# The tail of an AdaLN block: Sinkhorn renewed from exponent bits with its kernels in PSUM, branch output and residual added on GpSimd, ten of sixteen mix steps on TensorE

## The chip, the core and the metric

The kernel runs on one core of one Trainium2 chip. Five engines share the work: TensorE (PE in the profile) multiplies matrices into PSUM, VectorE (DVE), ScalarE (ACT) and GpSimd (POOL) work elementwise, and SyncE (SP) issues most DMA transfers. The metric is the device time of one launch in microseconds (us), the median of several runs. All data is 32-bit float.

## What is computed

The block takes x of 4 batches by 512 tokens by 1024 channels and adds two gated branches to it. The first is a Mamba-like branch (projection, convolution, selective scan, output projection). The second, which the change is about, is this, cut to what matters (C = 256 channels in each of n = 4 streams):

```python
x_norm = x * rsqrt(mean(x * x) + eps)                      # x: the modulated layer norm, "h" below
H_res_logits = (x_norm @ W_res.T).reshape(B, T, 4, 4) + H_res_base
H_res  = sinkhorn_log(H_res_logits)                        # 50 steps, tau = 0.1
H_pre  = softmax(x_norm @ W_pre.T + H_pre_base)
H_post = softmax(x_norm @ W_post.T + H_post_base)
H_res  = (1 - g) * I + g * H_res                           # g = sigmoid(gate)
x_pre  = einsum('btnc,btn->btc', x_streams, H_pre)
y      = x_pre @ W_branch
x_mixed       = einsum('btij,btjc->btic', H_res, x_streams)
y_distributed = einsum('btc,btn->btnc', y, H_post)
out = x + gb * (x_mixed + y_distributed)                   # x: the block's stream after the first branch
```

`sinkhorn_log` alternates u = -logsumexp over columns of Z + v and v = -logsumexp over rows of Z + u, 50 times, for one 4x4 matrix per token.

## The kernel before, in words

The 2048 tokens are 16 tiles of 128 tokens, one token to a partition. Everything up to the first branch's output lies in the first `with` block: eight blocks of 256 tokens, in each a selective scan of 64 steps on VectorE (L963) with TensorE, ScalarE (L933) and GpSimd (L917) feeding it. This part is ordered by hand (`manual_schedule`, L1003). It uses all eight PSUM banks: `ps_ht` 2, `ps_da` 2, `ps_mm` 4 (L104 to L106). `front` (L773) normalizes each tile for the second branch, stores it to DRAM (`h2_dram`) and leaves 24 logits per token in `lgs`: 16 for Sinkhorn, 4 for each softmax. The last two tiles' logits come at the very end of this block (L829).

The second `with` block (L1037) is the tail. Here the framework's scheduler orders the instructions of each engine when the kernel is built; an engine then runs its own list strictly in that order, and waits on semaphores for the others. The parts are:

- Loads (L1067, L1070): `h2` and `x1`, 16 tiles of 512 KB each, on SP's queue, and later a row of gb per batch, broadcast to all partitions (`gb_row`, L1047).
- `softmaxes` (L1074): H_pre and H_post.
- `sinkhorn` (L1088): in two parts, tiles 0 to 13 (part 0, tile names `sk`, `sa`, `sb`) and tiles 14 and 15 (part 1, `skl`). Instead of logarithms it scales: with kk = exp(z) and kt its transpose, each of 50 steps is product, row sum and reciprocal for u (L1131, L1132, L1133) and the same for v (L1135, L1136, L1137), six VectorE instructions. After steps 10, 20, 30 and 40 the scales are folded into z: ScalarE takes logarithms (L1140, L1141), VectorE adds them (L1142, L1143) and ScalarE makes kk and kt anew (L1122, L1123). All four tiles z, kk, kt, w lie in SBUF. Part 1 is begun beside part 0 at its step 16 and carried on between the mixes.
- `branch` (L1162), per tile: ScalarE writes four diagonal matrices from H_pre (L1158), TensorE multiplies with them to form x_pre transposed (L1172), then multiplies by W_branch (L1180); ScalarE copies y out (L1182).
- `mix` (L1185), per tile, needs H_res: output streams 0 and 1 on TensorE, ten matmuls with diagonals that ScalarE writes (L1196, L1197: eight for H_res, two for H_post times y); streams 2 and 3 by eight multiply-adds on VectorE into PSUM (L1204), begun from y times H_post by ScalarE (L1202). Then VectorE multiplies by gb (L1210, L1211), GpSimd adds x1 (L1212), SP stores (L1213).

Of the kernel before, what the change touches and what calls it, by code (L numbers as in the profile page):

```python
# [8 lines left out]

F32 = mybir.dt.float32  # L10
AF = mybir.ActivationFunctionType
# [11 lines left out]
TT = TB // P  # L23
# [13 lines left out]
NS, C = 4, 256  # L37
NL = NS * NS + 2 * NS
BT = T // P
NTT = B * BT  # L40
SINKHORN_ITERS = 50
ABSORB = 10
# [3 lines left out]
EPS_LN = 1e-05  # L46
EPS_FFN = 1.1920929e-07
SA, CA, GA, SB, CB, GB = range(6)


@with_exitstack
def adaln_block(
# [22 lines left out]
    vec, act, pool, pe = nc.vector, nc.scalar, nc.gpsimd, nc.tensor  # L75
# [20 lines left out]

    parts_of = [(0, NTT - TT), (NTT - TT, TT)]
    lgs = [const.tile([P, n, NL], F32, name=f"lg_{i}", tag=f"lg_{i}") for i, n in parts_of]
    sk = const.tile([P, 4, parts_of[0][1], NS, NS], F32, name="sk")

    with ExitStack() as ph:
        p1 = ph.enter_context(tc.tile_pool(name="p1", bufs=1))
        p2 = ph.enter_context(tc.tile_pool(name="p2", bufs=2))
# [899 lines left out]
        with tc.manual_schedule():  # L1003
# [5 lines left out]
            for k in range(NBLK):  # L1009
# [27 lines left out]
    with ExitStack() as ph:  # L1037
        p1 = ph.enter_context(tc.tile_pool(name="f1", bufs=1))
        p2 = ph.enter_context(tc.tile_pool(name="f2", bufs=2))
        ps_oa = ph.enter_context(tc.tile_pool(name="ps_oa", bufs=2, space=PSUM))  # L1040
        ps_ob = ph.enter_context(tc.tile_pool(name="ps_ob", bufs=2, space=PSUM))
        ps_tr = ph.enter_context(tc.tile_pool(name="ps_ft", bufs=2, space=PSUM))
        NM = NS // 2

        gbs = {}

        def gb_row(b):  # L1047

            if b not in gbs:
                gbs[b] = p2.tile([P, H], F32, name=f"row_gb_{b}", tag="row_gb")  # L1050
                load(gbs[b], row_dram[GB][b, :].partition_broadcast(P))
            return gbs[b]

# [34 lines left out]
        def sinkhorn(part, tiles):  # L1088

            n = parts_of[part][1]
            sh = [P, n, NS, NS]
            z, kk, kt, w = (tiles[:, m] for m in range(4))

            def small(name):
                return const.tile([P, n, NS], F32, name=f"{name}_{part}", tag=f"{name}_{part}")
# [10 lines left out]
            mx, sa, sb_ = small("mx"), small("sa"), small("sb")  # L1109
            vec.tensor_scalar(  # L1110
                z, lgs[part][:, :, : NS * NS].rearrange("p t (i j) -> p t i j", j=NS), INV_TAU,
                None, ALU.mult,
            )
            vec.tensor_reduce(mx, z, AX.X, ALU.max)
            vec.tensor_tensor(z, z, over_j(mx), ALU.subtract)
            act.activation(w, z, AF.Exp)
            vec.tensor_reduce(sa, w, AX.X, ALU.add)
            vec.tensor_reduce(mx, by_col(z), AX.X, ALU.max)
            vec.tensor_tensor(z, z, over_i(mx), ALU.subtract)

            def kernel_of():
                act.activation(kk, z, AF.Exp)  # L1122
                act.activation(kt, by_col(z), AF.Exp)  # L1123

            kernel_of()
            fresh = False
            for it in range(SINKHORN_ITERS):
                if fresh:
                    vec.tensor_reduce(sa, kk, AX.X, ALU.add)
                elif it:  # L1130
                    vec.tensor_tensor(w, kk, over_i(sb_), ALU.mult)  # L1131
                    vec.tensor_reduce(sa, w, AX.X, ALU.add)  # L1132
                vec.reciprocal(sa, sa)  # L1133

                vec.tensor_tensor(w, kt, over_i(sa), ALU.mult)  # L1135
                vec.tensor_reduce(sb_, w, AX.X, ALU.add)  # L1136
                vec.reciprocal(sb_, sb_)  # L1137
                fresh = it and it % ABSORB == 0
                if fresh:
# [6 lines left out]
            hr = kk  # L1146
            vec.tensor_tensor(w, w, over_j(sb_), ALU.mult)
            vec.tensor_scalar(hr, by_col(w), gt, None, ALU.mult)
            dg = hr.rearrange("p t i j -> p t (i j)")[:, :, 0 : NS * NS : NS + 1]
            vec.tensor_scalar(dg, dg, gm, None, ALU.add)  # L1150
# [9 lines left out]
        ybs = {}  # L1160

        def branch(i):  # L1162

            hpp = own(hpps, i)
            dg = p1.tile([P, NS, P], F32, name=f"dgx_{i}", tag="dgx", bufs=3)
            xt = ps_tr.tile([P, C // P, P], F32, name=f"pxt_{i}", tag="xt")
# [11 lines left out]
            py = ps_tr.tile([P, C], F32, name=f"pyb_{i}", tag="yb")  # L1178
            for j in range(C // P):
                pe.matmul(py, xs[:, j, :], wbr[:, j, :], start=(j == 0), stop=(j == C // P - 1))  # L1180
            yb = p1.tile([P, C], F32, name=f"yb_{i}", tag="yb", bufs=NTT)
            act.copy(yb, py)  # L1182
            ybs[i] = yb

        def mix(i):  # L1185


            b, r = divmod(i, BT)
            hpp, hres = own(hpps, i), own(hress, i)
            hs = [h2[:, i, n * C : (n + 1) * C] for n in range(NS)]  # L1190
            oa = ps_oa.tile([P, NM, C], F32, name=f"oa_{i}", tag="oa")
            ob = ps_ob.tile([P, NS - NM, C], F32, name=f"ob_{i}", tag="ob")
            dg = p1.tile([P, NM, NS + 1, P], F32, name=f"dg_{i}", tag="dg", bufs=2)
            for n in range(NM):
                for m in range(NS + 1):
                    diagonal(dg[:, n, m, :], hres[:, n, m : m + 1] if m < NS else hpp[:, 1, n : n + 1])  # L1196
                    pe.matmul(  # L1197
                        oa[:, n, :], dg[:, n, m, :], hs[m] if m < NS else ybs[i],
                        start=(m == 0), stop=(m == NS),
                    )  # L1200
            for n in range(NM, NS):
                act.activation(ob[:, n - NM, :], ybs[i], AF.Copy, scale=hpp[:, 1, n : n + 1])  # L1202
                for m in range(NS):
                    vec.scalar_tensor_tensor(  # L1204
                        ob[:, n - NM, :], hs[m], hres[:, n, m : m + 1], ob[:, n - NM, :],
                        ALU.mult, ALU.add,
                    )
            of = p1.tile([P, H], F32, name=f"o_{i}", tag="o", bufs=3)
            gb = gb_row(b)
            vec.tensor_tensor(of[:, : NM * C], oa.rearrange("p n c -> p (n c)"), gb[:, : NM * C], ALU.mult)  # L1210
            vec.tensor_tensor(of[:, NM * C :], ob.rearrange("p n c -> p (n c)"), gb[:, NM * C :], ALU.mult)  # L1211
# [10 lines left out]
        for it in range(SINKHORN_ITERS + 1):  # L1222
            next(early, None)
            if it == APART:
                softmaxes(1)
                for i in last:
                    branch(i)
                small = p1.tile([P, 4, TT, NS, NS], F32, name="skl")
                late = sinkhorn(1, small)
            if late:  # L1230
                next(late, None)
# [56 lines left out]
```

## Time and profile before

| | us |
|---|---|
| median of 3 runs | 2709.85 (2709.05 to 2709.86) |
| the profiled execution's own time | 2702.3 |
| its span, first to last instruction | 2700.5 |
| first Sinkhorn step of part 0 (L1133) | at 2412.6 |
| first diagonal of the tail (L1158) | at 2476.8 |
| first diagonal of the mix | at 2603.8 |
| last addition on GpSimd (L1212) ends | at 2696.8 |

Busy time over the span: PE 2408.1 us (89%), DVE 2361.0 (87%), ACT 1716.9 (64%), POOL 1731.8 (64%). A row of the timeline gives the start in us from the span's start, the time that the merged instructions took, the engine, the source line, the operation with output and inputs, and in brackets how long the engine had been idle before and what ended that. A group gives busy time, mean nanoseconds of one instruction, and idle time with its releasers. A row of the windows table gives busy time and number of instructions per engine in that stretch, the granted TensorE clock (1.00 is full), the DMA share and GB/s.

### The profile page before, as it was taken

How to read it: one execution, taken by the hardware profiler on the slowest of the kernel's cores; microseconds unless marked ns; L12 is line 12 of the kernel's file. 1: busy time of each engine (PE TensorE's matmuls, PEld its weight loads, DVE VectorE, ACT ScalarE, POOL GpSimd, SP SyncE). 2: the span in 40 equal slices, each digit the busy share in tenths (PEclk: the TensorE clock that was granted, in tenths of full speed). 3: DMA queues.
4: the chain of work that ended last, by engine and by line, in shares of the span. 5: the costliest groups of instructions: out<-in, count | busy, mean ns of one | idle time of the engine just before them, and what ended most of it. 6: DMA issues, size and time to landing. Idle time of an engine off the chain costs nothing. (4 is left out here: it accounts for less than half of the span.)

```text
span 2700.5 us, 39703 instructions
## 1 busy us (share of the span) xinstructions
PE 2408.1 (89%) x13392; PEld 2051.6 (76%) x13392; DVE 2361.0 (87%) x4451; ACT 1716.9 (64%) x3755; POOL 1731.8 (64%) x1167
## 2 busy tenths in 40 slices
PE   8999989999999989998999899998999899885446
PEld 8887478888788878887888788887888777675435
DVE  0349898999999999999999999999999899977898
ACT  0356567666776777667776776668666856633445
POOL 0146557777976688768766786779676977931014
PEclk9979989999999999999999999999999899896769
DMA  5432523333433343234333433333333323225302
GB/s 184 152 125 94 204 75 130 113 106 121 154 117 104 116 153 121 106 114 149 125 110 114 156 118 109 118 145 125 121 106 124 130 94 117 83 74 203 153 31 110
DMA packets 74347, 331.06 MB, mean 123 GB/s; under 512 B 8496, under 2 KB 25312, under 8 KB 47456
## 3 DMA queue, kind: packets, MB, share of 16 engines
q1 hardware_dynamic: 62784, 311.56, 32.1%
q10 hardware_dynamic: 11360, 16.96, 1.7%
q8 instruction: 107, 1.75, 0.3%
q14 instruction: 96, 0.79, 0.1%
HBM read 303.14 MB, written 25.35 MB: 122 GB/s over the span
## 5 line engine op out<-in xcount | busy, mean ns | idle before, releaser
L917 POOL TENSOR_TENSOR w<-u,b 128x1024 f32<-128x1024 f32 x512 | 1209.1, 2363 | 558.2 <-PE hq L943 413.5
L933 ACT ACTIVATE da<-dv,aneg 128x256 f32<-128x256 f32 x2048 | 971.5, 477 | 616.5 <-DVE w L963 571.5
L963 DVE TENSOR_TENSOR_SCAN w<-da,w 128x256 f32<-128x256 f32 x2048 | 1263.3, 667 | 69.5 <-ACT da L933 47.6
L952 DVE SCALAR_TENSOR_TENSOR acc<-hq,ss,acc 128x512 f32<-128x512 f32 x1024 | 724.6, 735 | 78.2 <-PE hq L943 73.1
L943 PE MATMUL hq<-ident,w 128*128 128x128 f32 x4096 | 644.1, 282 | 73.1 <-DVE acc L952 53.7
L943 PEld LDWEIGHTS hq<-ident,w 128*128 128x128 f32 x4096 | 511.8, 146 | 220.7 <-issue 57.7
L487 PE MATMUL pz<-w_z,ht 128*128 128x256 f32 x2048 | 517.2, 387 | 0.0
L439 PE MATMUL pp<-ht,w_x 128*128 128x259 f32 x2048 | 511.5, 387 | 0.0
L667 PE MATMUL po<-y,w_out 128*128 128x256 f32 x2048 | 496.2, 381 | 5.4 <-ACT dv L608 5.4
L439 PEld LDWEIGHTS pp<-ht,w_x 128*128 128x128 f32 x2048 | 372.1, 193 | 46.2 <-issue 0.4
L667 PEld LDWEIGHTS po<-y,w_out 128*128 128x128 f32 x2048 | 368.6, 191 | 46.5 <-ACT dv L608 6.9
L487 PEld LDWEIGHTS pz<-w_z,ht 128*128 128x128 f32 x2048 | 369.2, 195 | 36.5 <-issue 0.3
L455 DVE SCALAR_TENSOR_TENSOR xc<-pp,cw,xc 128x256 f32<-128x256 f32 x384 | 178.4, 464 | 31.8 <-ACT xc L448 30.7
L1212 POOL TENSOR_TENSOR o<-o,x 128x1024 f32<-128x1024 f32 x16 | 37.7, 2354 | 189.1 <-ACT dg L1158 142.2
L1197 PE MATMUL oa<-h,dg 128*128 128x256 f32 x256 | 62.8, 389 | 74.9 <-ACT dg L1158 69.5
L1197 PEld LDWEIGHTS oa<-h,dg 128*128 128x128 f32 x256 | 49.3, 195 | 84.1 <-ACT dg L1158 76.5
L467 POOL TENSOR_TENSOR xc<-xc,sx 128x1024 f32<-128x1024 f32 x32 | 75.5, 2358 | 42.8 <-ACT sx L465 42.8
L448 ACT ACTIVATE xc<-pp,cb,cw 128x256 f32<-128x256 f32 x128 | 71.3, 557 | 47.5 <-PE pp L439 47.4
L749 PE MATMUL py<-ident,acc 128*128 128x128 f32 x256 | 48.4, 324 | 54.7 <-ACT dv L608 28.3
L262 PEld LDWEIGHTS pm<-sc,w_mod 128*128 128x128 f32 x384 | 80.9, 323 | 9.0 <-DVE mv_a L358 9.0
L262 PE MATMUL pm<-sc,w_mod 128*128 128x4 f32 x384 | 79.5, 343 | 9.1 <-DMA w_mod<-wmod_dram 9.1
L749 PEld LDWEIGHTS py<-ident,acc 128*128 128x128 f32 x256 | 34.8, 167 | 67.2 <-ACT dv L608 25.2
(172 smaller groups left out, 2303.2 us busy)
## 6 DMA issues: line engine op xcount, KB each, us to landing
w_x<-in_w_dram SPq DMA_DIRECT2D x64, 1024.0 KB, 4.7
w_z<-in_w_dram SPq DMA_DIRECT2D x64, 1024.0 KB, 4.9
w_out<-out_w_dram SPq DMA_DIRECT2D x56, 1024.0 KB, 4.8
w_mod<-wmod_dram SPq DMA_DIRECT2D x24, 1024.0 KB, 4.8
b<-bcd SPq DMA_DIRECT2D x32, 512.0 KB, 3.8
xt<-x_dram SPq DMA_DIRECT2D x16, 512.0 KB, 8.2
xr<-x_dram SPq DMA_DIRECT2D x32, 256.0 KB, 5.1
x<-xr ACTq DMA_DIRECT2D x32, 256.0 KB, 2.5
```

The lines of the kernel that those rows point to most:

```text
L262: pe.matmul(pm[:, 2 * q + j, :], w[:, k, j * P : (j + 1) * P], sc[:, k, :], start=(k == 0), stop=(k == HC - 1),)
L439: pe.matmul(pp, w[:, h, j * P : (j + 1) * P], hts[k][:, h, :], start=(h == 0), stop=(h == HC - 1),)
L455: vec.scalar_tensor_tensor(xc[:, c, :], pp[:, tap : tap + TB], cw[:, i, tap : tap + 1], xc[:, c, :], ALU.mult, ALU.add,)
L487: pe.matmul(pz[:, t, :], hts[k][:, h, PAD + t * P : PAD + (t + 1) * P], w[:, h, :], start=(h == 0), stop=(h == HC - 1),)
L667: pe.matmul(po, w[:, d - lo, :], ys[k, d // QC][:, d % QC, :], start=(d == lo), stop=(d == hi - 1),)
L749: pe.transpose(py[:, j, t * P : (t + 1) * P], acc[:, t, c * P : (c + 1) * P], ident)
L917: pool.tensor_tensor(w, us[k, q], bts[k, n // NG][:, n % NG, :].unsqueeze(1).to_broadcast([P, QC, TB]), ALU.mult,)
L933: act.activation(da[:, j, :], dts[k, q][:, 2 * s + j, :], AF.Exp, scale=aneg[:, i, n : n + 1])
L943: pe.transpose(h[:, c * P : (c + 1) * P], ws[g][:, c, t * P : (t + 1) * P], ident)
L952: vec.scalar_tensor_tensor(acc[:, t, :], hqs.pop((g, t)), cts[k][:, t, n : n + 1], acc[:, t, :], ALU.mult, ALU.add,)
L963: vec.tensor_tensor_scan(w[:, c, :], das[g, c // 2][:, c % 2, :], w[:, c, :], 0.0, ALU.mult, ALU.add)
L1197: pe.matmul(oa[:, n, :], dg[:, n, m, :], hs[m] if m < NS else ybs[i], start=(m == 0), stop=(m == NS),)
```

## The change

Three edits, all in the tail.

**Sinkhorn.** kk and kt move from SBUF to a PSUM tile `kb` from a new pool `ps_kk`; the two scales are halves of one tile `ab`. The renewal takes only the power of two of each scale: VectorE masks the exponent bits (`bits`), turns them into a logarithm by one multiply-add (`low`), adds that to z, and leaves the mantissa of v's scale in place. The step after a renewal is therefore an ordinary one with a product. The result goes to a tile `hr` of its own.

**Branch.** y is no longer kept. ScalarE writes it four times, scaled by H_post, into `yn`; GpSimd multiplies `yn` by gb and adds it to `x1` in place. x_pre and y share one PSUM tile `pb`. The four gb rows have each a buffer of their own.

**Mix.** TensorE does the eight products of streams 0 and 1 and two of stream 2, whose diagonals GpSimd writes; ScalarE does one of stream 3; VectorE does the other five.

```diff
-    sk = const.tile([P, 4, parts_of[0][1], NS, NS], F32, name="sk")
+    sk = const.tile([P, 2, parts_of[0][1], NS, NS], F32, name="sk")
...
+        ps_kk = ph.enter_context(tc.tile_pool(name="ps_kk", bufs=1, space=PSUM))
...
-                gbs[b] = p2.tile([P, H], F32, name=f"row_gb_{b}", tag="row_gb")
+                gbs[b] = p1.tile([P, H], F32, name=f"row_gb_{b}")
...
-            z, kk, kt, w = (tiles[:, m] for m in range(4))
+            z, w = tiles[:, 0], tiles[:, 1]
+            kb = ps_kk.tile([P, 2, n, NS, NS], F32, name=f"kb_{part}", tag=f"kb_{part}")
+            kk, kt = kb[:, 0], kb[:, 1]
...
-                fresh = it and it % ABSORB == 0
-                if fresh:
-                    act.activation(sa, sa, AF.Ln)
-                    act.activation(sb_, sb_, AF.Ln)
-                    vec.tensor_tensor(z, z, over_j(sa), ALU.add)
-                    vec.tensor_tensor(z, z, over_i(sb_), ALU.add)
+                if it and it % ABSORB == 0:
+                    vec.tensor_scalar(bits, ab.bitcast(I32), EXPONENT, None, ALU.bitwise_and)
+                    vec.tensor_scalar(low, bits, LN2 / 2**23, -127 * LN2, ALU.mult, ALU.add)
+                    vec.tensor_tensor(z, z, over_j(low[:, 0]), ALU.add)
+                    vec.tensor_tensor(z, z, over_i(low[:, 1]), ALU.add)
                     kernel_of()
+                    sbi = sb_.bitcast(I32)
+                    vec.tensor_scalar(sbi, sbi, MANTISSA, ONE, ALU.bitwise_and, ALU.bitwise_or)
                 yield
...
-            yb = p1.tile([P, C], F32, name=f"yb_{i}", tag="yb", bufs=NTT)
-            act.copy(yb, py)
-            ybs[i] = yb
+            yn = p1.tile([P, NS, C], F32, name=f"yn_{i}", tag="yn", bufs=3)
+            for n in range(NS):
+                act.activation(yn[:, n, :], py, AF.Copy, scale=hpp[:, 1, n : n + 1])
+            yn = yn.rearrange("p n c -> p (n c)")
+            pool.tensor_tensor(yn, yn, gb_row(i // BT), ALU.mult)
+            pool.tensor_tensor(x1[:, i, :], x1[:, i, :], yn, ALU.add)
...
+            act.activation(ob[:, 1, :], hs[0], AF.Copy, scale=hres[:, 3, 0:1])
+            on_pe = [(n, m) for n in range(2) for m in range(NS)] + [(2, 0), (2, 1)]
+            for d, (n, m) in enumerate(on_pe):
+                if n == 2:
+                    pool.tensor_scalar(dg[:, d, :], ident, hres[:, n, m : m + 1], None, ALU.mult)
+                else:
+                    diagonal(dg[:, d, :], hres[:, n, m : m + 1])
+                pe.matmul(
+                    oa[:, n, :] if n < 2 else ob[:, 0, :], dg[:, d, :], hs[m],
+                    start=(m == 0), stop=(m == (NS - 1 if n < 2 else 1)),
+                )
+            for n, m in ((3, 1), (3, 2), (3, 3), (2, 2), (2, 3)):
+                o = ob[:, n - 2, :]
+                vec.scalar_tensor_tensor(o, hs[m], hres[:, n, m : m + 1], o, ALU.mult, ALU.add)
```

More of the change, by code (lines that the diff above doesn't have):

```diff
@@ L10 @@
 F32 = mybir.dt.float32
+I32 = mybir.dt.int32
 AF = mybir.ActivationFunctionType
@@ L48 @@
 SA, CA, GA, SB, CB, GB = range(6)
+EXPONENT, MANTISSA, ONE = 0x7F800000, 0x007FFFFF, 0x3F800000
+LN2 = 0.6931471805599453
 @with_exitstack
@@ L1042, in adaln_block @@
         ps_tr = ph.enter_context(tc.tile_pool(name="ps_ft", bufs=2, space=PSUM))
-        NM = NS // 2
+        ps_kk = ph.enter_context(tc.tile_pool(name="ps_kk", bufs=1, space=PSUM))
         gbs = {}
@@ L1094, in sinkhorn, with small @@
             sh = [P, n, NS, NS]
-            z, kk, kt, w = (tiles[:, m] for m in range(4))
-            def small(name):
-                return const.tile([P, n, NS], F32, name=f"{name}_{part}", tag=f"{name}_{part}")
+            z, w = tiles[:, 0], tiles[:, 1]
+            kb = ps_kk.tile([P, 2, n, NS, NS], F32, name=f"kb_{part}", tag=f"kb_{part}")
+            kk, kt = kb[:, 0], kb[:, 1]
+            def small(name, *lead, dtype=F32):
+                return const.tile(
+                    [P, *lead, n, NS], dtype, name=f"{name}_{part}", tag=f"{name}_{part}"
+                )
             def over_i(v):
@@ L1107, in by_col @@
                 return a.rearrange("p t i j -> p t j i")
-            mx, sa, sb_ = small("mx"), small("sa"), small("sb")
+            mx, ab, bits, low = small("mx"), small("ab", 2), small("bits", 2, dtype=I32), small("low", 2)
+            sa, sb_ = ab[:, 0], ab[:, 1]
             vec.tensor_scalar(
@@ L1125, in sinkhorn @@
             kernel_of()
-            fresh = False
             for it in range(SINKHORN_ITERS):
-                if fresh:
-                    vec.tensor_reduce(sa, kk, AX.X, ALU.add)
-                elif it:
+                if it:
                     vec.tensor_tensor(w, kk, over_i(sb_), ALU.mult)
@@ L1137, in sinkhorn @@
                 vec.reciprocal(sb_, sb_)
-                fresh = it and it % ABSORB == 0
-                if fresh:
-                    act.activation(sa, sa, AF.Ln)
-                    act.activation(sb_, sb_, AF.Ln)
-                    vec.tensor_tensor(z, z, over_j(sa), ALU.add)
-                    vec.tensor_tensor(z, z, over_i(sb_), ALU.add)
+                if it and it % ABSORB == 0:
[3 more added lines that the diff above has]
+                    vec.tensor_tensor(z, z, over_i(low[:, 1]), ALU.add)
                     kernel_of()
+                    sbi = sb_.bitcast(I32)
+                    vec.tensor_scalar(sbi, sbi, MANTISSA, ONE, ALU.bitwise_and, ALU.bitwise_or)
                 yield
-            hr = kk
+            hr = small("hr", NS)
+            hr = hr.rearrange("p i t j -> p t i j")
             vec.tensor_tensor(w, w, over_j(sb_), ALU.mult)
             vec.tensor_scalar(hr, by_col(w), gt, None, ALU.mult)
-            dg = hr.rearrange("p t i j -> p t (i j)")[:, :, 0 : NS * NS : NS + 1]
-            vec.tensor_scalar(dg, dg, gm, None, ALU.add)
+            for i in range(NS):
+                dg = hr[:, :, i, i]
+                vec.tensor_scalar(dg, dg, gm, None, ALU.add)
             hress[part] = hr
@@ L1158, in diagonal @@
             act.activation(dst, ident, AF.Copy, scale=coef)
-        ybs = {}
         def branch(i):
@@ L1165, in branch @@
             dg = p1.tile([P, NS, P], F32, name=f"dgx_{i}", tag="dgx", bufs=3)
-            xt = ps_tr.tile([P, C // P, P], F32, name=f"pxt_{i}", tag="xt")
+            pb = ps_tr.tile([P, 2, C], F32, name=f"pb_{i}", tag="pb")
+            xt, py = pb[:, 0].rearrange("p (j t) -> p j t", t=P), pb[:, 1]
             for n in range(NS):
@@ L1177, in branch @@
             act.copy(xs, xt)
-            py = ps_tr.tile([P, C], F32, name=f"pyb_{i}", tag="yb")
             for j in range(C // P):
                 pe.matmul(py, xs[:, j, :], wbr[:, j, :], start=(j == 0), stop=(j == C // P - 1))
-            yb = p1.tile([P, C], F32, name=f"yb_{i}", tag="yb", bufs=NTT)
-            act.copy(yb, py)
-            ybs[i] = yb
+            yn = p1.tile([P, NS, C], F32, name=f"yn_{i}", tag="yn", bufs=3)
+            for n in range(NS):
+                act.activation(yn[:, n, :], py, AF.Copy, scale=hpp[:, 1, n : n + 1])
@@ L1185, in mix @@
+            yn = yn.rearrange("p n c -> p (n c)")
+            pool.tensor_tensor(yn, yn, gb_row(i // BT), ALU.mult)
+            pool.tensor_tensor(x1[:, i, :], x1[:, i, :], yn, ALU.add)
         def mix(i):
             b, r = divmod(i, BT)
-            hpp, hres = own(hpps, i), own(hress, i)
+            hres = own(hress, i)
             hs = [h2[:, i, n * C : (n + 1) * C] for n in range(NS)]
-            oa = ps_oa.tile([P, NM, C], F32, name=f"oa_{i}", tag="oa")
-            ob = ps_ob.tile([P, NS - NM, C], F32, name=f"ob_{i}", tag="ob")
@@ L1193, in mix @@
[L1193 to L1207, printed above, removed]
+            oa = ps_oa.tile([P, 2, C], F32, name=f"oa_{i}", tag="oa")
@@ new lines, in mix @@
+            ob = ps_ob.tile([P, 2, C], F32, name=f"ob_{i}", tag="ob")
+            dg = p1.tile([P, 10, P], F32, name=f"dg_{i}", tag="dg", bufs=2)
+            act.activation(ob[:, 1, :], hs[0], AF.Copy, scale=hres[:, 3, 0:1])
[8 more added lines that the diff above has]
+                    start=(m == 0), stop=(m == (NS - 1 if n < 2 else 1)),
+                )
@@ L1208, in mix @@
+            for n, m in ((3, 1), (3, 2), (3, 3), (2, 2), (2, 3)):
+                o = ob[:, n - 2, :]
+                vec.scalar_tensor_tensor(o, hs[m], hres[:, n, m : m + 1], o, ALU.mult, ALU.add)
             of = p1.tile([P, H], F32, name=f"o_{i}", tag="o", bufs=3)
             gb = gb_row(b)
-            vec.tensor_tensor(of[:, : NM * C], oa.rearrange("p n c -> p (n c)"), gb[:, : NM * C], ALU.mult)
-            vec.tensor_tensor(of[:, NM * C :], ob.rearrange("p n c -> p (n c)"), gb[:, NM * C :], ALU.mult)
+            vec.tensor_tensor(of[:, : 2 * C], oa.rearrange("p n c -> p (n c)"), gb[:, : 2 * C], ALU.mult)
@@ L1212, in mix @@
+            vec.tensor_tensor(of[:, 2 * C :], ob.rearrange("p n c -> p (n c)"), gb[:, 2 * C :], ALU.mult)
             pool.tensor_tensor(of, of, x1[:, i, :], ALU.add)
@@ L1227, in adaln_block @@
                     branch(i)
-                small = p1.tile([P, 4, TT, NS, NS], F32, name="skl")
+                small = p1.tile([P, 2, TT, NS, NS], F32, name="skl")
                 late = sinkhorn(1, small)
```

## The prediction

> **What bounds the kernel now.** I read the windows of the tail first, then the timeline of its first 80 us, then the groups by form. The four stretches are: part 0's early Sinkhorn steps, the wait behind them, the rest of Sinkhorn, the mix.
>
> ```profile
> 2412.60:2460.50 47.90, 23.09 (x107) 18.83 (x106) 42.53 (x92) 4.88 (x7) 7.36 (x7) 0.73 0.32 110
> 2460.50:2481.00 20.50, 10.73 (x48) 9.93 (x48) 2.75 (x14) 11.99 (x28) 7.38 (x7) 0.50 0.26 99
> 2481.00:2603.80 122.80, 49.33 (x320) 46.27 (x320) 111.31 (x483) 50.38 (x129) 0.00 (x0) 0.68 0.35 140
> 2603.80:2700.50 96.70, 72.73 (x320) 61.75 (x320) 85.81 (x226) 63.78 (x194) 37.67 (x16) 0.91 0.24 98
> ```
>
> The columns after the length are PE, PEld, DVE, ACT, POOL. From 2481 to 2604 VectorE is busy 111 of 123 us while GpSimd does nothing: Sinkhorn alone sets that stretch. In the mix VectorE is busiest again (85.8 of 96.7). The timeline says when Sinkhorn runs:
>
> ```profile
> 2412.60 0.49 DVE L1133 RECIPROCAL sa<-sa 128x56 f32<-128x56 f32 x1
> ...
> 2460.03 0.50 DVE L1137 RECIPROCAL sb<-sb 128x56 f32<-128x56 f32 x1
> ...
> 2480.33 0.58 ACT L1123 ACTIVATE sk<-sk 128x224 f32<-128x224 f32 x1
> ...
> 2480.94 0.39 DVE L1135 TENSOR_TENSOR sk<-sk,sa 128x224 f32<-128x224 f32 x1 [2.56 <-ACT sk L1123]
> ...
> 2551.79 0.39 DVE L1131 TENSOR_TENSOR sk<-sk,sb 128x224 f32<-128x224 f32 x1
> ...
> 2554.56 0.39 DVE L1131 TENSOR_TENSOR sk<-sk,sb 128x224 f32<-128x224 f32 x1
> ```
>
> Steps 0 to 10 of part 0 are done by 2460, in gaps of VectorE while the first branch still ends. The first renewal waits for ScalarE until 2480.9; there step 11 goes on, with 39 of 50 steps left. One step takes 2554.56 - 2551.79 = 2.77 us, and part 1's step lies in the gaps of part 0's: alone, at 2446.0 to 2448.8, part 0 took 2.77 too. Half of step 11 (1.38) and 38 steps are 106.7 us; Sinkhorn ends at 2602.9, 122 later, so the last three renewals cost 15.3, 5.1 each (two table loads of 1.28 on ScalarE in each part's renewal).
>
> **Part by part.**
>
> *Kernels in PSUM: a later start.* Before the tail all eight banks belong to the scan's pools, so kb has no bank until those close. The instruction order of the changed kernel, as built, agrees: ScalarE's first exponential into kb stands behind the last logits' copies and 12 branch diagonals, and VectorE's first product with kb behind the last logits. Before, the twelve diagonals filled 2476.80 to 2480.4 and the exponential of kt followed. Now kk, a softmax exponential and kt follow, 0.5 us more: the first product comes at 2481.4 instead of step 11's at 2480.9. Eleven steps are lost.
>
> What the early steps cost there comes back: three instructions at 2415.9 to 2417.7 lay between the last sums of the scan (1.0 us), and two between the last tile's statistics at 2451 to 2453 (0.7). I take 1.5 us; the ends are 0.5 and 4, since others stood within 0.4 us of critical ones. First product: 2480.0.
>
> *The steps.* Both parts now start together. Each step still has six instructions of part 0, only two of them with an operand in PSUM. [...] the SBUF product L1131 takes 391 ns for 224 elements and 169 for 32, which extends to 724 at 512, and a product that reads PSUM takes less there:
>
> ```profile
> L1204 DVE SCALAR_TENSOR_TENSOR ob<-h,sk,ob 128x256 f32<-128x256 f32 x112 | 49.7, 479 | 0.4 <-ACT ob L1202 0.3
> ...
> L1210 DVE TENSOR_TENSOR o<-oa,row_gb 128x512 f32<-128x512 f32 x16 | 10.9, 684 | 3.9 <-DMA out_dram<-o 2.9 <-PE oa L1197 0.9
> ```
>
> By the row the pace stays 2.77[...]. I take the row: 1.38 + 49 x 2.77 = 137.1 us.
>
> *Renewals.* No logarithm and no table load, but five VectorE instructions (two on 112 elements, one on 56, two additions of 224) and again two exponentials. With ScalarE and GpSimd idle: about 1.6 us for the five and part 1's pieces between them, 0.5 for kk, 0.7 until part 1's kk; 3 us against 5.1 before. That holds for renewals 1 and 4.
>
> Renewals 2 and 3 meet the new GpSimd work. Its 32 products and additions take 2.36 us each (L917, L1212), 75.5 in all, and they are queued behind the gb rows, which SP issues after all h2 and x1 loads. Before, the rows were issued at 2513.3, with the DMA share at 1.0 until 2522 and 0 from 2524; so GpSimd starts at about 2520.5. From then it runs back to back, and a VectorE instruction with two SBUF inputs, or a plain one on SBUF, waits each time for the running one to end:
>
> ```profile
> 327.62 2.35 POOL L735 TENSOR_TENSOR acc<-acc,sz 128x1024 f32<-128x1024 f32 x1
> 328.25 1.86 DVE L246 TENSOR_SCALAR mr<-mr 4x256 f32<-4x256 f32 x1
> 329.93 2.40 POOL L917 TENSOR_TENSOR w<-u,b 128x1024 f32<-128x1024 f32 x1
> 330.04 2.42 DVE L247 TENSOR_SCALAR mr<-mr 4x256 f32<-4x256 f32 x1
> ```
>
> L247 needs nothing of L246; it lost 2.4 us because GpSimd's next one got in first. The step's own products, with one operand in PSUM, should be free of this, as L1210 is. The renewals' masks and additions are not. Step 20 ends at 2480.0 + 1.4 + 10 x 2.77 + 3 + 27.7 = 2539.8. There GpSimd has work that needs nothing more from ScalarE until about 2549 (12 instructions from 2520.5), so z is ready at about 2550 and not 2542. Then kt stands on ScalarE behind yn's four writes (1.6), a copy (0.4) and four diagonals (1.3): it comes at 2554.4, where the unbroken step would have had it at 2541.2; part 1 adds 1. That is 14 us (6 if nothing blocks). Step 30 ends at 2581.5; GpSimd is backlogged from 2552 to 2600. If every one of part 0's five pays a turn, 12 us, and 2.5 for part 1's: 14; if only the two-input additions do, 9.5; free, 3. No row shows an integer mask, so I take 12. The four renewals: 3 + 14 + 12 + 3 = 32 (15 free, 35 at most).
>
> *Branch.* ScalarE goes from 2.2 to 3.5 us per tile (four writes of 0.4 for one copy), 56 us inside a stretch that lasts 170; yn's three buffers hold it to GpSimd's 4.7 us per tile, done at 2600. Hidden, except for the queue order priced above. H_res: one more product and four small adds, 1.7 us. The mix begins at 2480.0 + 137.1 + 32 + 1.7 = 2650.8, against 2603.8: **47 us later**.
>
> *Mix.* TensorE's ten matmuls per tile stay ten (two of y go, two of stream 2 come); its cadence is two of these groups per tile:
>
> ```profile
> 2650.29 1.89 PE L1197 MATMUL oa<-h,dg 128*128 128x256 f32 x8
> ...
> 2652.45 1.89 PE L1197 MATMUL oa<-h,dg 128*128 128x256 f32 x8
> ```
>
> 2.16 us per five matmuls, 4.32 per tile. VectorE drops from eight multiply-adds to five: 5 x 0.48 + 2 x 0.61 = 3.6 us, and part 1's steps (about 20 us of VectorE's 85.8) are no longer in this stretch. ScalarE needs 8 x 0.30 + 0.45 = 2.9. GpSimd: 2.36 and two diagonals of 128 elements, for which no row exists; 128-element products take 0.40 (L552), 2-element scalings 0.23, so 0.5 to 0.8 for both: 3.2. TensorE becomes the bound: 0.8 to the first matmul, 2.2 for its low clock at the start (the first eight took 3.78 instead of 1.89 before), 16 x 4.32 = 69.1, 3.0 for the last tile's multiply-adds and product, 6.2 from there to the end as before (2694.3 to 2700.5): 81.3, against 96.7. **15.4 us shorter**.
>
> *Sum.* 2650.8 + 81.3 = 2732.1 against the span of 2700.5: +31.6. The profiled execution took 2702.3 with what lies around its span, the median of the runs is 7.5 us above that. I put the difference on the median: 2709.85 + 31.6 = 2741.
>
> **Rivals.** *The blocking doesn't bite* (GpSimd yields between its turns, or it is late and idle at steps 20 and 30). For it: in the tail of before single products waited for one turn only (L1135 at 2457.92, 1.65 us). Against: L247. Renewals cost 15, the sum is +15: 2724. *A PSUM source costs more*[...]. *A quicker step*, on the other side: the step is a chain in which each instruction starts 0.42 after the one that it needs, while independent ones start 0.31 apart (2540.14 to 2540.56); if reading kb from PSUM shortened that latency, the pace would fall. Each 0.1 us is worth 4.9; it decides from a pace of 2.77 - 31.6/49 = 2.13, and at 1.8 the kernel would be 16 faster: 2694. Against it: part 1's instructions fill the gaps already and the products' operand w is still written to and read from SBUF. *The gain of the mix is not there* (a GpSimd diagonal of 1 us, or DMA): 5 us up at most.
>
> **How the numbers follow.** Later start with blocking 0.61 (2741, own range 2732 to 2750); without blocking 0.22 (2724); dearer PSUM 0.08[...]; quicker step, faster, 0.05; quicker step that just balances 0.04. The range takes in the free renewals, the 4 us end of the early saving[...]: 2721 to 2757. A measurement of this kernel can tell about 0.2% (5.4 us) from no change. Slower by more than that 0.91, within it 0.04, faster 0.05.
>
> **What would show it.** The first product with kb at about 2480, no Sinkhorn step before it; 2.7 to 2.8 us between steps; VectorE masks and additions of over 2 us at renewals 2 and 3, ended by GpSimd; kt of renewal 2 late behind yn; the mix's start near 2651 and TensorE without gaps in it, 4.3 us per tile. A pace under 2.3, or a product with kb before 2470, would make the prediction wrong.

## The result, and the profile after

The changed kernel takes 2739.7 us (median of 4 runs, 2733.8 to 2741.4) against 2709.85: slower by a factor of 1.0104, 95% interval 1.009 to 1.0119. The profiled execution took 2741.4, its span is 2739.6. The prediction was 2741.

Line numbers after are 3 to 10 above those before: products L1136 and L1140, sums L1137 and L1141, reciprocals L1138 and L1142, mask L1144, multiply-add L1145, additions L1146 and L1147, exponentials L1130 and L1131, yn's writes L1190, GpSimd's two instructions L1192 and L1193, mix L1204 to L1222.

The spans mislead at first: they differ by 39.1 us, the medians by 29.9. Where the two profiled executions part is seen on an instruction that both kernels have, with the same work ahead of it: the last product w of the scan on GpSimd, of which there are 512. In the timeline of the kernel before:

```profile
2404.61 2.36 POOL L917 TENSOR_TENSOR w<-u,b 128x1024 f32<-128x1024 f32 x1 [1.66 <-PE hq L943]
```

In the changed kernel it starts at 2414.16, 9.55 later, though nothing ahead of it was changed. In the twelve profiles of this study it starts between 2402.1 and 2415.9, so this part of the kernel alone varies by 14 us from one execution to another. From here on all stages are counted from that instruction. To the end of the span it is 295.9 us before and 325.4 after: +29.5, as the medians say.

The stretches of the changed kernel's windows table, with the columns of the tables before (PE, PEld, DVE, ACT, POOL, clock, DMA share, GB/s); they begin at that product, at the first diagonal and at the mix:

```profile
2414.20:2482.60 68.40, 38.27 (x186) 32.45 (x184) 23.92 (x44) 12.96 (x23) 17.05 (x15) 0.75 0.27 96
2482.60:2657.80 175.20, 53.81 (x320) 48.75 (x320) 166.65 (x643) 54.95 (x167) 75.06 (x32) 0.66 0.27 110
2657.80:2739.60 81.80, 71.37 (x320) 62.18 (x320) 64.16 (x129) 46.52 (x144) 56.51 (x48) 0.94 0.25 103
```

The same three stretches before are 72.2, 127.0 and 96.7. So 3.7 us are won ahead of the tail, 48 are lost in Sinkhorn, 15 are won in the mix. In the second stretch GpSimd now has its 32 instructions (75 us), where before it had none. The timeline of the changed kernel shows the parts:

```profile
2487.15 0.39 DVE L1140 TENSOR_TENSOR sk<-kb,ab 128x224 f32<-128x224 f32 x1
...
2509.49 0.39 DVE L1140 TENSOR_TENSOR sk<-kb,ab 128x224 f32<-128x224 f32 x1
...
2512.26 0.39 DVE L1140 TENSOR_TENSOR sk<-kb,ab 128x224 f32<-128x224 f32 x1
...
2543.38 4.67 POOL L1193 TENSOR_TENSOR x<-x,yn 128x1024 f32<-128x1024 f32 x2
...
2544.18 0.39 DVE L1137 TENSOR_REDUCE ab<-sk 128x56 f32<-128x224 f32 x1
...
2546.52 3.87 DVE L1144 TENSOR_SCALAR bits<-ab 128x112 int32<-128x112 int32 x2
...
2555.79 0.36 ACT L1130 ACTIVATE kb<-sk 128x224 f32<-128x224 f32 x1 [7.00 <-DVE sk L1147]
2556.08 1.55 ACT L1190 ACTIVATE yn<-pb,hpp 128x256 f32<-128x256 f32 x4
...
2558.95 0.58 ACT L1131 ACTIVATE kb<-sk 128x224 f32<-128x224 f32 x1
...
2559.56 0.39 DVE L1136 TENSOR_TENSOR sk<-kb,ab 128x224 f32<-128x224 f32 x1 [1.55 <-ACT kb L1131]
```

The first row is the first product of part 0 in the tail, the first half of step 0; the two below it are a step apart, 2.77 us. The rest is renewal 2. GpSimd is at work from 2543.38 to 2548.05 with two instructions of 2.36, and the sum at 2544.18, inside the first of them, takes its usual 0.39. The masks of both parts take 3.87 together: the first (1.60) ends when GpSimd's second instruction has ended, the second (2.35) when GpSimd's next one has. kk is made at 2555.8, kt only at 2558.95, behind the four writes of yn. In the mix, from the same timeline:

```profile
2703.93 3.62 PE L1211 MATMUL oa<-h,dg 128*128 128x256 f32 x16
...
2707.38 1.03 PE L1211 MATMUL ob<-h,dg 128*128 128x256 f32 x4
...
2708.24 3.62 PE L1211 MATMUL oa<-h,dg 128*128 128x256 f32 x16
```

A tile lasts 4.31 us on TensorE, without a gap.

### The profile page after: what moved, and what is told of

Read it like the earlier page. It is cut to its first block, busy times and chain, and to the rows that moved or that the text cites. A ratio compares the mean times of both kernels' runs of the same rounds, so it can differ in the third digit from the quotient of the medians.

```text
span 2739.6 us, 39804 instructions
## 1 busy us (share of the span) xinstructions
PE 2414.7 (88%) x13392; PEld 2058.6 (75%) x13392; DVE 2367.8 (86%) x4441; ACT 1696.1 (62%) x3723; POOL 1825.9 (67%) x1231
## 5 line engine op out<-in xcount | busy, mean ns | idle before, releaser
L946 PE MATMUL hq<-ident,w 128*128 128x128 f32 x4096 | 647.1, 283 | 77.2 <-DVE acc L955 57.2
L507 POOL TENSOR_TENSOR sz<-sz,sgz 128x512 f32<-128x512 f32 x64 | 81.7, 1276 | 6.8 <-ACT sgz L505 6.8
L1180 PE MATMUL pb<-dgx,h 128*128 128x128 f32 x256 | 40.8, 316 | 50.9 <-ACT yn L1190 45.3
L738 POOL TENSOR_TENSOR acc<-acc,sz 128x1024 f32<-128x1024 f32 x32 | 75.5, 2359 | 11.9 <-DVE acc L955 11.8
```

Of the source, the lines that this page charges most:

```text
L507: pool.tensor_tensor(sz[:, :, s, :], sz[:, :, s, :], sg, ALU.mult)
L946: pe.transpose(h[:, c * P : (c + 1) * P], ws[g][:, c, t * P : (t + 1) * P], ident)
```

## Experiments

The theory was the prediction's (later start, renewals blocked by GpSimd, mix bound by TensorE). The rivals: a PSUM operand makes the steps dearer; masks are slow of themselves; the later start costs nothing. The table has all kernels. Stages are in us and from each profile: from the scan's last product to the first diagonal, on to the mix, and the mix to the end; "tail" is their sum. Ratios are to the kernel before, in runs on the same chip, with 95% intervals; a median is of 4 to 12 runs (one in the kernel with eight steps).

| kernel | to first diagonal | to mix | mix | tail | median | ratio |
|---|---|---|---|---|---|---|
| before | 72.2 | 127.0 | 96.7 | 295.9 | | |
| changed | 68.5 | 175.1 | 81.8 | 325.4 | 2739.7 | 1.0104 (1.009 to 1.0119) |
| early steps | 72.3 | 144.1 | 81.8 | 298.2 | 2711.9 | 1.0009 (0.9995 to 1.0023) |
| no GpSimd in branch | 68.8 | 159.9 | 82.5 | 311.2 | 2723.3 | 1.0058 (1.0038 to 1.0079) |
| scales in PSUM | 68.9 | 165.7 | 81.2 | 315.8 | 2732.4 | 1.0085 (1.0059 to 1.011) |
| old Sinkhorn | 72.6 | 174.0 | 87.7 | 334.3 | 2744.3 | 1.0141 (1.0113 to 1.0168) |
| eight on TensorE | 68.6 | 173.9 | 71.6 | 314.1 | 2727.0 | one run |
| early and scales | 72.1 | 135.9 | 82.6 | 290.6 | 2704.4 | 0.9978 (0.9968 to 0.9988) |
| the same and order | 72.1 | 135.4 | 82.9 | 290.3 | 2701.9 | 0.9975 (0.9964 to 0.9987) |
| powers of two alone | 72.8 | 119.2 | 98.8 | 290.8 | 2703.0 | 0.9971 (0.996 to 0.9982) |
| early, scales, eight | 72.5 | 135.6 | 80.0 | 288.1 | 2699.5 | 0.9967 (0.9955 to 0.9979) |
| early, scales, eight, order | 72.0 | 130.3 | 80.0 | 282.3 | 2699.3 | 0.9965 (0.9952 to 0.9978) |

### The early steps given back

```diff
-            kb = ps_kk.tile([P, 2, n, NS, NS], F32, ...)
-            kk, kt = kb[:, 0], kb[:, 1]
+            kk, kt = in_psum() if part else (tiles[:, 2], tiles[:, 3])   # in_psum: a kb tile as before
...
+                    if it == ABSORB and not part:
+                        kk, kt = in_psum()
                     kernel_of(kk, kt)
```

(`bits`, `low` and `hr` move to the tail's own pool to make room for the two tiles.)

> The changed kernel, but part 0 keeps its first kk and kt in SBUF and moves to the PSUM tile kb only at the first renewal. So steps 0 to 10 can run beside the end of the first branch again. Theory (the later start is the largest loss: 11 steps of 2.77 less what they cost the front): the first product with kb comes about 5 us later than in the changed kernel, but as step 11 and not step 1; the mix begins some 25 to 28 us earlier, the time is 2712 (2706 to 2718), pace still 2.77. Rival (the later start is no loss, the steps ahead of the tail only delayed the front by as much as they saved): no gain over 2740, more than 2733. Rival (a PSUM operand is what makes the kernel slower): pace unchanged against the changed kernel, so only the 25 us of the start are seen in either case; told apart by the pace of part 0 before and after its first renewal, 2.77 against 2.77 (theory) or above 2.9.

Measured: 2711.9, as the theory had it; the tail is 27.2 shorter than in the changed kernel. The window of its profile from the first diagonal to the mix:

```profile
2483.50:2627.70 144.20, 55.54 (x320) 50.01 (x320) 139.41 (x512) 53.71 (x163) 75.21 (x32) 0.69 0.33 133
```

This stretch is 31.0 shorter than in the changed kernel, the one before it 3.7 longer, the mix the same (81.8). VectorE has 131 instructions fewer in the stretch. This single edit takes back nearly all of the loss, and the kernel is level with the one before. The blocking has no part in that gain: GpSimd's turns now meet renewals 3 and 4, which cost 12.4 and 10.5. An undisturbed step of part 0 takes 2.77 before its first renewal with SBUF operands (2452.24 to 2455.01) and 2.77 after it with PSUM (2518.30 to 2521.07): the rival of the dear PSUM operand is out.

### GpSimd's work left out

```diff
-            pool.tensor_tensor(yn, yn, gb_row(i // BT), ALU.mult)
-            pool.tensor_tensor(x1[:, i, :], x1[:, i, :], yn, ALU.add)
+            gb_row(i // BT)
```

> The changed kernel without the two GpSimd instructions of the branch: y is not added to the output (left out: gb times y times H_post). The gb rows are loaded as before. Theory (renewals 2 and 3 are long because VectorE's masks and additions wait for GpSimd's turns): renewals 2 and 3 of part 0 fall from 13 and 10 us to 3 (4 where kt stands behind other work of ScalarE), part 1's from 2.3 to under 1; no VectorE instruction over 1 us there; the stretch from the first diagonal to the mix is 18 to 23 us shorter, the time about 2719. Rival (integer masks and conversions are slow of themselves): the stretch keeps within 3 us. Rival (only kt's place behind yn's writes counts): 4 us shorter at most.

Measured: 15.2 off the stretch to the mix, less than the 18 to 23 expected. By the starts of part 0's second reciprocals, renewals 2, 3 and 4 cost 2.4 us each over a step's 2.77 (13.0, 10.2 and 2.4 in the changed kernel), and nothing of part 1's renewals is seen in part 0. That part of the theory holds. Slow masks are out (renewal 2's takes 0.22, last row below), and so is the rival that only kt's place counts, which allowed 4 us. But renewal 1 rose from 2.4 to 10.2. The timeline of this kernel there:

```profile
2513.02 0.39 DVE L1147 TENSOR_TENSOR sk<-sk,low 128x224 f32<-128x224 f32 x1
...
2518.28 0.37 ACT L1130 ACTIVATE kb<-sk 128x224 f32<-128x224 f32 x1
...
2521.58 0.58 ACT L1131 ACTIVATE kb<-sk 128x224 f32<-128x224 f32 x1
...
2522.19 0.39 DVE L1136 TENSOR_TENSOR sk<-kb,ab 128x224 f32<-128x224 f32 x1 [8.24 <-ACT kb L1131]
...
2549.86 0.22 DVE L1144 TENSOR_SCALAR bits<-ab 128x112 int32<-128x112 int32 x1
```

z is ready at 2513.4; kk waits until 2518.3 and kt until 2521.6, since ScalarE, which here never waits for a yn buffer, has the branch's writes, copies and diagonals ahead of them in its fixed order. The queue order alone cost this renewal 7.7 us, more than the prediction gave it, and hid as much of what leaving GpSimd's work out had won.

### The scales in PSUM

```diff
+        scales = ps_kk.tile([P, 512], F32, name="scales")
...
-            mx, ab, bits, low = small("mx"), small("ab", 2), small("bits", 2, dtype=I32), small("low", 2)
+            mx, ab, bits, low = small("mx"), small("ab", 2), in_bank(64, 288), in_bank(176, 304)
+            bits = bits.bitcast(I32)
```

(`in_bank` cuts its piece out of `scales`, which also holds part 1's kernels; eight banks are all in use.)

> The changed kernel with bits and low in PSUM (one bank shared with part 1's kernels). The additions to z then have one operand in SBUF and one in PSUM, like the products; the multiply-add reads and writes PSUM; the mask still reads SBUF. Theory (what waits for GpSimd is an instruction with two SBUF inputs, or a plain one from SBUF to SBUF): the additions and the multiply-add take 0.4 us in renewals 2 and 3 too; if the mask still waits, one turn of 2.4 each for part 0 and part 1 remains: stretch from the first diagonal to the mix 12 to 20 us shorter, time 2720 to 2728. Rival (any VectorE instruction that touches SBUF as output or input waits in a renewal): no change beyond 3 us.

Measured: 9.4 off the stretch; the profiled run's tail falls by 9.6. Below the lower end of 12 that was expected, and 2732.4 lies above the expected 2720 to 2728. The mask of renewal 2 and then renewal 3 in this kernel's timeline:

```profile
2543.74 4.66 POOL L1202 TENSOR_TENSOR x<-x,yn 128x1024 f32<-128x1024 f32 x2
...
2547.57 0.28 DVE L1153 TENSOR_SCALAR scales<-ab 128x112 int32<-128x112 int32 x1
...
2588.70 0.28 DVE L1154 TENSOR_SCALAR scales<-scales 128x112 f32<-128x112 int32 x1
2588.72 2.34 POOL L1202 TENSOR_TENSOR x<-x,yn 128x1024 f32<-128x1024 f32 x1
2588.89 2.22 DVE L1159 TENSOR_SCALAR ab<-ab 128x56 int32<-128x56 int32 x1
...
2591.02 2.36 POOL L1201 TENSOR_TENSOR yn<-yn,row_gb 128x1024 f32<-128x1024 f32 x1
2591.03 0.37 DVE L1155 TENSOR_TENSOR sk<-sk,scales 128x224 f32<-128x224 f32 x1
```

The mask from SBUF to PSUM takes 0.28, well inside GpSimd's work, which lasts to 2548.40; the one from SBUF to SBUF took 1.60 in the changed kernel's renewal 2 and 1.79 in its renewal 3. There the multiply-add and the first addition of renewal 3 took 2.27 and 2.47; here they take 0.28 and 0.37, the addition inside GpSimd's turn. Only the mantissa's mask, still from SBUF to SBUF, waits (2.22). So the theory of the blocking holds to the operand. What ate part of the gain is order: renewal 2 still costs 7.5, as kt stands behind yn, and part 0 loses 5.0 in a later step behind a product of part 1, whose exponential is behind yn in turn.

### Before's Sinkhorn beside the new branch

The whole function `sinkhorn` is that of the kernel before, with kk and kt in SBUF; branch and mix are the changed ones.

> Before's Sinkhorn (logarithms, all four tiles in SBUF, steps 0 to 10 ahead of the tail) with the changed branch and mix: GpSimd's 32 turns of the branch then run beside products with two SBUF inputs. Theory: in GpSimd's 75 us each product waits a turn while sums and reciprocals go on, so a step of part 0 takes at least 4.7 us (two turns), up to 9.4 if part 1's two products take turns of their own, instead of 2.77; 31 to 53 us are lost against the kernel before and the mix gives 15 back: 2726 to 2748. Rival (products do not wait; the blocking is a matter of the masks alone): pace 2.77 throughout, 2709.9 - 15 = 2695. Either way the mix takes 81 to 83 us from its first ScalarE instruction, not 96.7.

Measured: 2744.3, within the range; the tail is 38.4 longer than before. In GpSimd's stretch steps of part 0 take up to 10 us, several of them 9.5 (timeline of this kernel):

```profile
2577.00 1.64 DVE L1137 TENSOR_TENSOR sk<-sk,sa 128x224 f32<-128x224 f32 x1
2578.47 2.38 POOL L1187 TENSOR_TENSOR x<-x,yn 128x1024 f32<-128x1024 f32 x1
2578.56 2.34 DVE L1133 TENSOR_TENSOR skl<-skl,sb 128x32 f32<-128x32 f32 x1
...
2581.77 1.65 DVE L1133 TENSOR_TENSOR sk<-sk,sb 128x224 f32<-128x224 f32 x1
```

Each of the two products of part 0 and the two of part 1 waits for a GpSimd instruction to end, even the one of 32 elements (2.34); sums and reciprocals don't (0.37 and 0.50 at 2576.05 and 2576.46, inside an instruction of GpSimd). So PSUM for kk and kt is no mistake of the change: with GpSimd at work beside Sinkhorn, the kernel with early steps, whose kb lies in PSUM from the first renewal on, has a tail 36 us shorter (298.2 against 334.3; its renewal differs too). What costs is that PSUM was used from step 0 on. The mix is 87.7 and not 81 to 83 as expected, with part 1's last steps in it.

### Eight mix steps on TensorE

```diff
-            on_pe = [(n, m) for n in range(2) for m in range(NS)] + [(2, 0), (2, 1)]
+            act.activation(ob[:, 0, :], hs[0], AF.Copy, scale=hres[:, 2, 0:1])
+            on_pe = [(n, m) for n in range(2) for m in range(NS)]
...
-            for n, m in ((3, 1), (3, 2), (3, 3), (2, 2), (2, 3)):
+            for n, m in ((3, 1), (3, 2), (3, 3), (2, 1), (2, 2), (2, 3)):
```

> The changed kernel with eight instead of ten mix steps on TensorE: stream 2 is begun by ScalarE and takes three multiply-adds on VectorE (six per tile in all), GpSimd writes no diagonals. Theory (TensorE bounds the mix at 4.32 us per tile, VectorE is close behind): TensorE needs 3.46, VectorE 6 x 0.49 + 2 x 0.69 = 4.3 to 4.5 becomes the bound, so the mix takes 81 to 85 us, about what it takes now. Then most of the mix's gain over before comes from y leaving it, little from the two steps on TensorE. Rival (TensorE's two steps are what saves the time): the mix takes over 88 us.

Measured: the mix takes 71.6, ten less than with ten steps on TensorE, and neither the theory nor the rival had that. This kernel ran once, so its time of 2727.0 carries no interval; the mix is read within its profile. Both bounds worked out for it were off: VectorE was put at 4.3 to 4.5 us per tile, and it isn't. The first row below is the changed kernel's, the others this one's: two of its timeline, a group of its tail (busy time and mean ns behind the bar), and the middle of its mix as a window:

```profile
2699.88 2.59 DVE L1217 SCALAR_TENSOR_TENSOR ob<-h,hr,ob 128x256 f32<-128x256 f32 x5 [0.18 <-PE ob L1211]
...
2687.10 2.06 DVE L1218 SCALAR_TENSOR_TENSOR ob<-h,hr,ob 128x256 f32<-128x256 f32 x5 [0.17 <-ACT ob L1205]
...
L1218 DVE SCALAR_TENSOR_TENSOR ob<-h,hr,ob 128x256 f32<-128x256 f32 x96 | 41.8, 481 | 1.8 <-ACT ob L1205 1.6
...
2660.00:2715.00 55.00, 53.28 (x244) 45.73 (x242) 52.03 (x114) 45.69 (x141) 32.79 (x14) 1.00 0.31 125
```

In the changed kernel five multiply-adds start 0.525 us apart and take 2.59; here five take 2.06 (starts 0.39 apart), as one begins before the record of the one ahead of it ends. So 96 with a mean of 481 ns cover 41.8 us, 435 ns each, and the 80 of the changed kernel 39.2. Per tile the six cover only 0.16 us more than the five did; why they start closer together here is not shown. The two matmuls that replaced the sixth cost TensorE, the bound, 0.86 (two tenths of 4.31), of which 0.64 per tile came off the mix. TensorE is still the busiest engine here (53.3 of 55.0), with VectorE close behind (52.0). In this respect the change did too much: with eight, its mix gains 25 and not 15.

### Combinations

Early steps together with the scales in PSUM:

> The early steps (part 0's first kk and kt in SBUF, kb from the first renewal on) together with bits and low in PSUM. Theory: renewals 3 and 4 of part 0, which now meet GpSimd's turns (12.4 and 10.5 us in the kernel with the early steps alone), lose the blocking of mask, multiply-add and additions; what stays is kt behind yn's writes and the mask of the mantissa, which still goes from SBUF to SBUF: 5 to 8 us each. First diagonal to mix 133 to 139 us against 144.1, time 2700 to 2706 against 2708 for the kernel before. Rival (the blocking only moves on to the next instruction with two SBUF inputs): no gain over the early steps alone, 2712.

Measured: 2704.4, ratio 0.9978; 8.2 off the stretch to the mix against the early steps alone. As expected.

In addition, part 0's Sinkhorn from step 10 on is emitted at high priority:

```diff
+            if it >= ABSORB:
+                with tc.high_priority():
+                    next(early, None)
```

> As the kernel with early steps and scales in PSUM, and in addition the scheduler is told to put part 0's Sinkhorn instructions from step 10 on ahead of others where both are ready, so that the two exponentials of a renewal are no longer behind yn's writes and part 1's steps don't stand ahead of part 0's. Theory (what is left of renewals 2 to 4 is queue order): each renewal of part 0 costs 2.4 to 4.8 us, first diagonal to mix 122 to 130 us, time 2691 to 2698: faster than both. Rival (putting part 0 ahead starves the branch of ScalarE, so yn and GpSimd end later and the mix waits for x1 or for part 1): Sinkhorn shorter but the mix longer by as much.

Measured: 2701.9, and a stretch of 135.4 instead of 135.9: the expected 122 to 130 are missed. Renewal 3 does fall, from 8.9 to 3.3 (renewal 2 stays at 2.5). But another step now takes 11.1, and renewal 4 rises from 5.1 to 9.0. The timeline shows why:

```profile
2570.36 0.21 ACT L1143 ACTIVATE scales<-skl 128x32 f32<-128x32 f32 x1
...
2572.22 1.57 ACT L1205 ACTIVATE yn<-pb,hpp 128x256 f32<-128x256 f32 x4 [1.64 <-POOL x L1208]
...
2574.20 0.19 DVE L1149 TENSOR_TENSOR skl<-scales,ab 128x32 f32<-128x32 f32 x1 [8.30 <-ACT scales L1144]
```

Part 1's exponential (the one of kt ends at 2574.2) is behind a yn write that waits for GpSimd to free a buffer; part 1's product waits for it; and part 0's next product is behind that one on VectorE. The expectation had looked at part 0's queue only.

The new renewal alone, in the kernel before:

> The kernel before with only the renewal changed: powers of two instead of logarithms, all tiles in SBUF, early steps kept, branch and mix as before, so GpSimd does nothing beside Sinkhorn. Theory (the new renewal is cheaper when nothing blocks it): 2.4 to 3 us per renewal of part 0, if the exponentials aren't behind the branch's work on ScalarE, against 5.1 before; 5 to 9 us less in all, 2699 to 2704 against 2708. Rival (the kernel before hides its logarithms beside other work already): no difference, 2706 to 2710.

Measured: 2703.0, ratio 0.9971; the stretch to the mix falls from 127.0 to 119.2, the mix is 2.1 longer. Renewals 2 to 4 of part 0 cost 2.4, 1.9 and 1.9. So the new renewal by itself, with GpSimd idle beside it, is a gain.

Early steps, scales and eight steps on TensorE:

> Early steps, bits and low in PSUM, and eight mix steps on TensorE (six multiply-adds on VectorE, no diagonals on GpSimd). Theory: the gains add: the mix takes 72 to 75 us instead of 82.6 (part 1's last steps lie in it), Sinkhorn as in the kernel with early steps and scales in PSUM; 2704 less 8 to 10 = 2694 to 2696, faster than both kernels. Rival (with part 1's steps still in the mix VectorE, now at 3.7 of 3.5 us per tile, becomes the bound): mix 78 or more, no better than 2700.

Measured: 2699.5, but the mix takes 80.0 and not 72 to 75. The rival holds. The window of this kernel while part 1 is still in the mix:

```profile
2615.10:2675.50 60.40, 53.61 (x224) 45.23 (x224) 57.24 (x213) 46.23 (x142) 28.30 (x12) 0.92 0.24 96
```

VectorE is busy 57.2 of 60.4: with part 0 starting early, part 1 has 17 of its 50 steps left at the mix, and they use up most of what the two steps would have given.

The last one puts both parts ahead and gives yn four buffers:

> As the kernel with early steps, scales in PSUM and eight steps on TensorE, and both parts' Sinkhorn from step 10 on put ahead by the scheduler, with four yn buffers instead of three, so that ScalarE stands less often waiting for GpSimd with an exponential behind it. Theory (what is left over 2.4 us per renewal is an exponential queued behind a yn write that waits for a buffer): renewals 2 to 4 of part 0 and the stall of part 0 behind part 1's third renewal shrink by 5 to 12 us in all: 2684 to 2690. Rival (the order only decides which renewal stands behind a yn write, as in the kernel where part 0 alone was put ahead): no difference to the kernel without the new order, 2692 to 2697.

Measured: the stretch is 5.3 shorter, the tail in the profile 5.8, at the lower end of what was expected, but the medians (2699.3 and 2699.5) don't separate the two; the forecast of 2684 to 2690 had taken the mix at its 72. The run changes order and buffers at once and doesn't tell them apart. The two last kernels have the lowest medians of the study, 0.3% below the kernel before; their intervals overlap with that of the new renewal alone.

## Why the prediction held, point by point

It was right in time and in its main mechanism. That 2739.7 came within 2 us of 2741 is partly luck: the four runs spread over 7.6 us, the interval of the ratio is worth 24 to 32 us, and errors of both signs cancelled in part. The numbers below are counted from the scan's last product.

- *Later start.* Predicted: no step ahead of the tail, first product at 2480.0. Measured: 2487.15 - 9.55 = 2477.6. The wait from the first diagonal to it is 4.5, as worked out. Off was what the early steps had cost: 1.5 was taken, within 0.5 to 4. All kernels without them take 68.5 to 68.9 to the first diagonal, all with them 72.0 to 72.8: **3.6**. That term was too small by 2.1. Giving the steps back shows the net loss, 27 us.
- *The steps.* Pace 2.77 predicted and measured. The product takes 391 ns with one operand, kb, in PSUM, as it did with both in SBUF. The row decided rightly; the upper end of the range, 2757, allowed for a dearer PSUM operand, which was not shown by any row. (Of the rows named for the quicker step, those 0.31 apart start at 2540.25 and 2540.56; from 2540.14 it is 0.42. Nothing hung on it.)
- *Renewals.* 32 predicted. Measured for part 0: 2.4, 13.0, 10.2 and 2.4, and twice 2.3 for part 1's: 32.6. The division was nearly right too (renewals 2 and 3, each with part 1's: 14 and 12 predicted, 15.3 and 12.4 measured). That GpSimd causes them is shown by the run without its work and by the scales in PSUM. Two things were too broad: of plain instructions on SBUF only masks and multiply-adds wait (up to 2.35 and 2.31), sums and reciprocals don't (at most 0.39 and 0.50); and of part 0's five in renewal 3 four waited (1.79, 2.27, 2.47, 2.42), while the mantissa's mask fell between two of GpSimd's instructions (0.18). And kt behind yn was priced for renewal 2 alone: the later runs show that order on ScalarE costs up to 8 us a renewal once the blocking is gone.
- *Branch hidden*: yes, but for the queue order. GpSimd begins at 2529.5 - 9.55 = 2520.0; predicted 2520.5.
- *H_res*: 0.9 instead of 1.7.
- *Mix.* 81.3 predicted, 81.8 measured; 4.31 per tile. The two diagonals on GpSimd take 1.19 and not 0.5 to 0.8, which costs nothing, as GpSimd was not the bound. That TensorE is the bound is shown by two steps taken from it (one run), and by part 1: with ten steps on TensorE and the new Sinkhorn the mix takes 81.2 to 82.9 in all six kernels, whether 1 of part 1's steps lies in it (changed kernel), 12 (early steps) or 17 (scales in PSUM). So part 1's leaving the mix, which the prediction counted in VectorE's favour, gave nothing here; with eight steps on TensorE it decides between 71.6 and 80.0.
- *Sum.* +31.6 predicted, +29.5 in the tail: -2.4 from the front, -0.8 from H_res, +0.6 from renewals and +0.5 from the mix. Put together from the runs, the 48 us lost between first diagonal and mix are 31.0 for the early steps and 17 more: what renewals 2 and 3 cost beyond 2.4 each, part 1's share included (22.9), less roughly 6 that the cheaper renewal gives back (7.8 in the run with the new renewal alone).
- *Rivals.* No blocking (2724), dearer PSUM, a quicker step (2694) and no gain in the mix are all contradicted by rows above.

Left open: why the unchanged part ahead of the tail varies by 14 us between executions, which no run looks into, and how far order could still be improved beyond the last kernel.

## What to carry to other kernels

Ask of every buffer that moves to PSUM not only what its operand costs but when a bank first becomes free: work that was hidden ahead of a stage boundary is lost if its buffer can't exist there (here eleven steps, worth 31.0 us between first diagonal and mix). Before putting GpSimd beside a chain of small VectorE instructions, look which of them read two SBUF operands or go from SBUF to SBUF; in these runs the products, additions, masks and multiply-adds of that kind, where they met a running GpSimd instruction, waited for its end, up to 2.5 us whatever their own size, and one operand in PSUM freed them (a mask 0.28, an addition 0.37, a product 0.39). When a step is moved from one engine to another, add up the time that the instructions cover together, not their mean durations: in the kernel with eight steps on TensorE, 96 multiply-adds with a mean of 481 ns covered 435 each.

## What the runs showed that was not expected

- A mask from SBUF to PSUM isn't held up by GpSimd (0.28 us), one from SBUF to SBUF is (1.6 to 2.3); sums and reciprocals from SBUF to SBUF aren't either (at most 0.39 and 0.50 where they start inside a GpSimd instruction of the changed kernel).
- Two matmuls cost TensorE 0.86 us per tile and left VectorE's multiply-adds only 0.16 us shorter.
- Taking GpSimd's work away made one renewal 7.7 us longer, as ScalarE then ran ahead with the branch and put the exponentials behind it.
